# Side work of a two-layer graph-attention kernel issued as 32-column matmuls, four beside each other

## Chip, cores and metric

The kernel runs on one core of a Trainium2 chip. The metric is the device time of one execution in microseconds (us); before the change it is 4478.36 us, the median of 3 runs (4476.70 to 4484.94). All data and all matmuls spoken of here are 32-bit floats unless a line says otherwise.

## What is computed

Input `x` has 8 batches of 2048 rows by 256 features; `adj` is one 2048 x 2048 mask for all batches. Two layers follow each other, each on the normalised and rectified rows of the layer before, each with 4 heads of 64.

```python
# layer 0
h = relu(layernorm(x))
q, k, v = h @ Wq.T + bq, h @ Wk.T + bk, h @ Wv.T + bv        # 4 heads of 64
scores = where(mask == 0, -10, clip(q . k / 8, -10, 10))     # keys in chunks of 256
ctx = sum over chunks of softmax(scores in the chunk) @ v
x = x + (layernorm(ctx @ Wo.T + bo + h) * gamma + beta)
# layer 1
h = relu(layernorm(x));  q = h @ W                            # 4 heads of 64
e = leaky(q . a_src [row] + q . a_dst [column], 0.2)
x = x + elu(softmax(where(mask, e, -9e15)) @ q)
```

## The kernel before

Layer 0 runs over 256 steps (`steps`: 8 batches, 4 blocks of 512 queries, 8 chunks of 256 keys). In each step TensorE makes the scores of a step that lies two ahead (`scores`, L396, contraction over 64 rows, two heads beside each other), VectorE clips and masks them (L404), ScalarE takes the exponential (L410), GpSimd adds two key tiles (L680), and TensorE multiplies the exponentials of the present step with `v` (`weigh`, L416) and sums them with ones (`add_up`, L427). These last two are matmuls with only 32 columns of weights. Four of them are issued in a row, one for each head, and write partitions 0-31, 32-63, 64-95 and 96-127 of the same accumulator. The sums go to ScalarE (L434), through DRAM (`divide`, `spread`) and come back as a factor `r`, with which VectorE scales the contexts (`accumulate`, L452).

Layer 1 runs over 32 passes (8 batches, 2 pairs of heads, 2 halves of the rows) of 16 rounds (`rounds`). A round makes two tiles of weights on VectorE (`clipped`, L761), contexts on TensorE (`weigh_rows`, L772, again four matmuls of 32 columns beside each other), and every second round a sum of them (ScalarE L874, GpSimd L878, TensorE `add_up_rows`, L784).

Everything else is side work, written as generators that wait in a list `aside`. `advance()` lets one or several of them take their next piece, and the main loops call it at fixed places: in layer 0 twice in a step, once after the first half of the contexts (between L416 and the next L396) and once after the second half; in layer 1 once in a round. The order on every engine is the order in which the program issues, so that a piece of side work stands in each engine's queue just where `advance()` was called. The side work on TensorE is:

- `turn` (L171): four 128 x 128 transposes of a normalised row pair into `hT`, 64 times in each layer; ScalarE copies the result (L172).
- `block` (L297): the projections to q and k, two matmuls of 128 columns of weights and 512 moving columns for each half, 128 times in layer 0 (16 of them at the start, before the steps). ScalarE copies the result (L304).
- `sides` (L191): four matmuls with 256 moving columns, 64 times for v in layer 0 (ScalarE copies, L314) and 64 times for q of layer 1 (VectorE multiplies, L629).
- `finish` (L479): four matmuls with 256 moving columns for the output projection of layer 0, 64 times (VectorE adds, L487).
- `preparation` (L599): four transposes, 8 times; `ending` (L805, four transposes of the sums, 32 times; VectorE takes their reciprocal at L807) and (L815, four transposes of the contexts, 64 times; VectorE L818).
- a small matmul in `preparation` (L559), which has 32 columns of weights already and 128 moving columns.

All side work shares one accumulator (`aux`, one buffer after the start), so that a piece waits until the copy of the piece before it is done. At the last pass of each batch of layer 1, `drain` issues what is left of the next batch's preparation, its last L191 pieces among it, in a row.

The lines of the side work before are full matmuls or transposes with all 128 columns of weights, as here in `sides`:

```python
            for ic in range(FC):
                nc.tensor.matmul(
                    ps[:, u, :],
                    hT[:, ic, t * P : (t + 1) * P],
                    rhs[:, ic, :],
```

Of the kernel before, what the change touches and what calls it, by code (L numbers as in the profile page):

```python
# [16 lines left out]
P = 128  # L17
# [34 lines left out]
def layers(  # L52
# [18 lines left out]
    nc = tc.nc  # L71
# [81 lines left out]
    def normal(xb, blk, two, norm):  # L153
# [9 lines left out]
            hs.append(h)  # L163
        return hs

    def turn(hs, two, hT):

        ps = aux().rearrange("p (t c r) -> p c t r", t=2, c=FC)
        for u in range(2):
            for c in range(FC):  # L170
                nc.tensor.transpose(ps[:, c, u, :], hs[u][:, c * P : (c + 1) * P], ident)  # L171
        nc.scalar.copy(  # L172
            hT[:, :, two * 256 : (two + 1) * 256].rearrange("p c (t r) -> p c t r", t=2), ps
        )
# [10 lines left out]
    def sides(rhs, two, hT):  # L185

        ps = aux().rearrange("p (t f) -> p t f", t=2)
        for u in range(2):
            t = 2 * two + u
            for ic in range(FC):  # L190
                nc.tensor.matmul(  # L191
                    ps[:, u, :],
                    hT[:, ic, t * P : (t + 1) * P],
                    rhs[:, ic, :],
                    start=(ic == 0),
                    stop=(ic == FC - 1),
                )
        return ps
# [78 lines left out]
    def block(b, blk, xb, qs, ks, vs):  # L277

        first = b and (b - 1) * NQB * NCH

        while b and here[0] < first + (NCH, 2 * NCH, 3 * NCH, 4 * NCH - 2)[blk]:
            yield False
        while b == 1 and len(made) < NQB:
            yield False
        if b and blk == 0:
            yield True
        hT = big.tile([P, FC, QB], F32, tag="hT", name="hT", bufs=1)
        yield from block_turned(xb, blk, norm_of[b], hT)
        for name, to in (("q", qs), ("k", ks)):
            if name == "q":  # L290
                r = big.tile([P, FC, QB], F32, tag="q", name="qT", bufs=4)
            else:
                r = big.tile([P, FC, QB], F32, tag="kv", name="kT", bufs=12)
            for oc in range(FC):
                ps = aux()
                for ic in range(FC):
                    nc.tensor.matmul(  # L297
                        ps,
                        wT[name][:, ic, oc * P : (oc + 1) * P],
                        hT[:, ic, :],  # L300
                        start=(ic == 0),
                        stop=(ic == FC - 1),
                    )
                nc.scalar.activation(  # L304
                    r[:, oc, :], ps, AF.Identity, bias=bcol[name][:, oc : oc + 1], scale=PART[name]
                )
                if oc == FC - 1:
                    to.append(r)
                yield
        while b and here[0] < first + (0, 0, 3 * NCH + 2, 3 * NCH + 4)[blk]:  # L310
            yield False
        r = big.tile([P, NT, F], F32, tag="kv", name="v", bufs=12)
        for two in range(NT // 2):
            nc.scalar.copy(r[:, 2 * two : 2 * two + 2, :], sides(wT["v"], two, hT))  # L314
            if two == 1:
                vs.append(r)
            yield
# [24 lines left out]
    for name, w in (("q", Wq), ("k", Wk), ("v", Wv), ("o", Wo)):  # L342
# [14 lines left out]
        for ic in range(FC):  # L357
            ps = aux()[:, :F]
# [97 lines left out]
    def finish(b, qb, acc):  # L456
        rstd, off = norm_of[b]
        xb = load(x[b], qb)
        n = here[0]

        while here[0] < n + 1:
            yield False
        o = big.tile([P, NT, F], F32, tag="o", name="o")
        for t in range(NT):
            i = qb * NT + t
            nc.scalar.activation(
                o[:, t, :], xb[:, t, :], AF.Relu, scale=rstd[:, i : i + 1], bias=off[:, i : i + 1]
            )
        nc.gpsimd.tensor_tensor(o, o, bcast(brow["o"], 1, NT), ALU.add)
        yield True  # L470
        while here[0] < n + 2:
            yield False
        mv = small.tile([P, NT, 2], F32, tag="mv2", name="mv2")
        for two in range(NT // 2):
            ps = aux().rearrange("p (t f) -> p t f", t=2)
            for u in range(2):
                t = 2 * two + u
                for part in range(2):
                    nc.tensor.matmul(  # L479
                        ps[:, u, :],  # L480
                        acc[:, part, t * P : (t + 1) * P],
                        wT["o"][:, part, :],
                        start=(part == 0),
                        stop=(part == 1),
                    )
            mine = o[:, 2 * two : 2 * two + 2, :]
            nc.vector.tensor_tensor(mine, mine, ps, ALU.add)  # L487
            yield
            for u in range(2):
                t = 2 * two + u  # L490
                row_stats(nc, small, mv[:, t, :], o[:, t, :])
        rstd2 = small.tile([P, NT], F32, tag="rstd2", name="rstd2")
        off2 = small.tile([P, NT], F32, tag="off2", name="off2")
        roots(mv, rstd2, off2, slice(0, NT))
        yield True
        offsets(rstd2, off2, slice(0, NT))
        n = here[0]
        while here[0] < n + 1:
            yield False
        for t in range(NT):  # L500
            nc.scalar.activation(
                o[:, t, :], o[:, t, :], AF.Identity,
                scale=rstd2[:, t : t + 1], bias=off2[:, t : t + 1],
            )
            if t == 1:
                yield True
        for k, more in enumerate((bcast(brow["gamma"], 1, NT), bcast(brow["beta"], 1, NT), xb)):
            yield True
            n = here[0]
            while here[0] < n + 1:  # L510
                yield False
            nc.gpsimd.tensor_tensor(o, o, more, ALU.add if k else ALU.mult)
        nc.gpsimd.dma_start(
            x1[b][qb * QB : (qb + 1) * QB, :].rearrange("(t p) f -> p t f", p=P), o
        )
        yield True
# [27 lines left out]
    def preparation(b):  # L544
# [4 lines left out]
        er = const.tile([P, NQB, P], F32, tag="wv", name="er")  # L549
# [46 lines left out]
        yield True  # L596
        ps = aux().rearrange("p (b k) -> p b k", k=P)
        for blk in range(NQB):
            nc.tensor.transpose(ps[:, blk, :], er[:, blk, :], ident)  # L599
        ed = ps.rearrange("p b (c k) -> p (b c) k", k=32)[:, :, H : 2 * H]  # L600
        far = small.tile([P, NKT, H], F32, tag="far", name="far")
        nc.vector.scalar_tensor_tensor(far, ed, -0.8, bcast(off_s, 1, NKT), ALU.mult, ALU.add)
# [193 lines left out]
    def ending(k, cT, dT):  # L796

        b, hp, half = passes[k]
        xs = big.tile([P, 2, NT, P], F32, tag="acc", name="xh")
        for blk in range(2):  # L800
            nc.sync.dma_start(xs[:, blk, :, :], mine(x1[b], 2 * half + blk, hp))
        yield True
        ps = aux().rearrange("p (c k) -> p c k", c=NT)
        for c in range(NT):
            nc.tensor.transpose(ps[:, c, :], dT[:, c * P : (c + 1) * P], ident)  # L805
        r = small.tile([P, 2, NT, 2], F32, tag="inverse", name="inverse")
        nc.vector.reciprocal(r, ps.rearrange("p c (h b k) -> p b c h k", h=2, b=2)[:, :, :, :, 0])  # L807
        nc.vector.tensor_reduce(
            inverse_most[:, k : k + 1], r.rearrange("p b c h -> p (b c h)"), mybir.AxisListType.X, ALU.max
        )  # L810
        yield
        for blk in range(2):
            ps = aux().rearrange("p (t f) -> p t f", t=NT)
            for t in range(NT):
                nc.tensor.transpose(ps[:, t, :], cT[:, blk, t * P : (t + 1) * P], ident)  # L815
            both = big.tile([P, 2, NT, P], F32, tag="c", name="z")
            z, low = both[:, 0, :, :], both[:, 1, :, :]
            nc.vector.tensor_tensor(  # L818
                z.rearrange("p t (h d) -> p (t h) d", h=2),
                ps.rearrange("p t (h d) -> p (t h) d", h=2),  # L820
                bcast(r[:, blk, :, :].rearrange("p c h -> p (c h)"), 2, DH),
                ALU.mult,
            )
            yield

            xh = xs[:, blk, :, :]
            nc.scalar.activation(low, z, AF.Relu, scale=-1.0)
            nc.scalar.activation(low, low, AF.Exp, scale=-1.0)
            nc.scalar.activation(z, z, AF.Relu)
            nc.scalar.activation(xh, xh, AF.Copy, bias=-1.0)  # L830
            yield True
            nc.gpsimd.tensor_tensor(z, z, low, ALU.add)
            nc.gpsimd.tensor_tensor(xh, xh, z, ALU.add)
            yield True
            nc.sync.dma_start(mine(out[b], 2 * half + blk, hp), xh)
# [365 lines left out]
```

## Time and profile before

| | us |
|---|---|
| median of 3 runs | 4478.36 (4476.70 to 4484.94) |
| the profiled execution | 4470.84, of which span 4469.0 |
| layer 0 in the trace (starts of the first and last of its sums, L427) | 126 to 2885 |
| layer 1 in the trace (starts of the first and last L761) | 2908.5 to 4444.4 |

The mean granted clock of TensorE is 0.991. In the trace a 32-bit matmul leaves two records for its matmul and two for its weight load; a transpose leaves one of each. The groups of the side work on TensorE, with the columns "busy us, mean ns of one | idle before, and its releaser":

```profile
L479 PE MATMUL aux<-wo,acc 128*128 128x256 f32 x512 | 128.2, 393 | 0.0
L191 PE MATMUL aux<-wv,hT 128*128 128x256 f32 x512 | 126.1, 390 | 0.0
L297 PE MATMUL aux<-hT,wk 128*128 128x512 f32 x256 | 125.5, 615 | 0.0
L171 PE MATMUL aux<-ident,h 128*128 128x128 f32 x512 | 92.3, 297 | 28.4 <-ACT h L160 27.3
L815 PE MATMUL aux<-ident,cT 128*128 128x128 f32 x256 | 42.3, 288 | 1.1 <-DVE z L818 0.8 <-DVE inverse L807 0.4
L805 PE MATMUL aux<-ident,dT 128*128 128x128 f32 x128 | 21.0, 286 | 0.7 <-ACT dT L892 0.7
L559 PE MATMUL aux<-hT,wa 128*32 128x128 f32 x512 | 20.5, 273 | 0.0
```

The form "128*128" is rows times columns of the weights; "128x256" is partitions by moving columns. A duration holds the time that a matmul spends passing through the array, which overlaps the next one, so what a block of them costs is read from start to start, not from these means.

### The profile page before, as it was taken

To read this page: it belongs to the slowest core of one execution; us is meant where nothing else is said; L and a number is where in the kernel's file an instruction comes from. 1 tells how busy PE (TensorE), PEld (TensorE's weight loads), DVE (VectorE), ACT (ScalarE), POOL (GpSimd) and SP (SyncE) were. 2 spreads that over 40 slices of the span, in tenths; PEclk is the share of its full clock that TensorE was granted. 3 is DMA by queue.
4 is the path that set the end of the run, shared out by engine and by line. 5 is a ranking of instruction groups with operands and counts; after the bars stand their busy time and mean duration, and the time that the engine had idled before them with its cause. 6 is when DMAs were issued, how large, how long until landed. Compare 5 with 4: busy or idle time off the path is not lost. (4 is left out here: it accounts for less than half of the span.)

```text
span 4469.0 us, 73769 instructions
## 1 busy us (share of the span) xinstructions
PE 4235.0 (95%) x28598; PEld 1462.8 (33%) x28598; DVE 3157.1 (71%) x3736; ACT 2712.5 (61%) x3454; POOL 3275.9 (73%) x1558
## 2 busy tenths in 40 slices
PE   6799999999999999999999999989999999999998
PEld 3233333323323333333333333323233332323332
DVE  1775566566565565575565566588989889898987
ACT  4766556656655665665656557565647566565755
POOL 0477787787677777777777777777877777787877
PEclk8999999999999999999999999999999999999999
DMA  2421121111121121121111122121221212122111
GB/s 70 140 62 44 43 66 47 43 56 56 35 64 54 37 66 44 46 64 44 47 55 50 40 64 61 44 100 50 72 63 60 78 57 86 52 74 62 59 55 35
DMA packets 295000, 262.03 MB, mean 59 GB/s; under 512 B 96240, under 2 KB 245488, under 8 KB 294640
## 3 DMA queue, kind: packets, MB, share of 16 engines
q1 hardware_dynamic: 290032, 240.45, 18.8%
q0 software_dynamic: 4608, 16.78, 1.0%
q8 instruction: 226, 3.70, 0.3%
q14 instruction: 134, 1.10, 0.1%
HBM read 218.83 MB, written 36.18 MB: 57 GB/s over the span
## 5 line engine op out<-in xcount | busy, mean ns | idle before, releaser
L680 POOL TENSOR_TENSOR add<-E 128x1024 f32<-128x1024 f32 x512 | 1201.3, 2369 | 721.9 <-PE sums L427 532.1
L410 ACT ACTIVATE E<-E 128x1024 f32<-128x1024 f32 x1024 | 1080.5, 1057 | 827.3 <-DVE E L404 809.6
L404 DVE SCALAR_TENSOR_TENSOR E<-big,limit 128x1024 f32<-128x1024 f32 x1024 | 1203.7, 1217 | 521.6 <-PE big L396 515.5
L761 DVE SCALAR_TENSOR_TENSOR e<-near,far,limit 128x1024 f32<-128x1024 f32 x1024 | 1240.0, 1273 | 23.2 <-ACT near L750 9.8
L878 POOL TENSOR_TENSOR t<-t,e 128x1024 f32<-128x1024 f32 x448 | 1054.4, 2387 | 246.0 <-ACT t L874 210.4
L416 PE MATMUL both<-E,v 128*32 128x512 f32 x8192 | 1037.7, 601 | 59.8 <-DVE c L452 42.3
L772 PE MATMUL acc<-e,qn 128*32 128x512 f32 x8192 | 1060.7, 597 | 24.4 <-DVE e L761 13.5
L396 PE MATMUL big<-qT,kT 64*128 64x512 f32 x4096 | 1032.3, 620 | 11.8 <-DVE E L404 11.8
L874 ACT ACTIVATE t<-e,quot 128x1024 f32<-128x1024 f32 x512 | 561.2, 1142 | 313.5 <-PE den L784 173.0
L396 PEld LDWEIGHTS big<-qT,kT 64*128 64x128 f32 x4096 | 351.6, 187 | 572.0 <-issue 348.8
L454 POOL TENSOR_TENSOR acc<-acc,c 128x1024 f32<-128x1024 f32 x224 | 532.9, 2379 | 3.6 <-DVE c L452 3.6
L452 DVE TENSOR_TENSOR c<-both,r 128x1024 f32<-128x1024 f32 x224 | 274.2, 1224 | 345.9 <-PE both L416 157.1
L416 PEld LDWEIGHTS both<-E,v 128*32 128x32 f32 x8192 | 214.7, 109 | 752.3 <-issue 572.8
L772 PEld LDWEIGHTS acc<-e,qn 128*32 128x32 f32 x8192 | 259.2, 109 | 591.5 <-issue 451.1
L784 PE MATMUL den<-t,for_sums 128*32 128x512 f32 x2048 | 347.6, 595 | 30.6 <-POOL t L878 29.8
L427 PE MATMUL sums<-add,ones 128*32 128x512 f32 x2048 | 269.1, 592 | 0.2 <-POOL add L680 0.2
L434 ACT COPY s<-sums 128x512 f32<-128x512 f32 x256 | 148.4, 580 | 75.5 <-PE sums L427 71.3
L784 PEld LDWEIGHTS den<-t,for_sums 128*32 128x32 f32 x2048 | 79.2, 110 | 223.1 <-issue 113.3
L191 PE MATMUL aux<-w,hT 128*128 128x256 f32 x512 | 127.6, 392 | 22.6 <-DVE qn L629 22.6
L160 ACT ACTIVATE h<-x,off,rstd 128x256 f32<-128x256 f32 x256 | 139.2, 593 | 4.3 <-DMA x<-in_x_dram 2.3
L297 PE MATMUL aux<-hT,wq 128*128 128x512 f32 x256 | 135.7, 658 | 2.7 <-ACT hT L172 2.7
L479 PE MATMUL aux<-wo,acc 128*128 128x256 f32 x512 | 128.2, 393 | 0.0
(117 smaller groups left out, 3033.8 us busy)
## 6 DMA issues: line engine op xcount, KB each, us to landing
r<-inv SPq DMA_DIRECT2D x1024, 64.0 KB
x<-in_x_dram SPq DMA_DIRECT2D x92, 512.0 KB
x<-x SPq DMA_DIRECT2D x64, 512.0 KB
es<-er SPq DMA_DIRECT2D x64, 512.0 KB
adj_in<-in_adj_dram SPq DMA_DIRECT2D x32, 512.0 KB
x<-o POOLq DMA_DIRECT2D x32, 512.0 KB, 3.9
xh<-x SPq DMA_DIRECT2D x64, 256.0 KB
out_dram<-xh SPq DMA_DIRECT2D x64, 256.0 KB
```

What stands on the lines that cost most here:

```text
L396: nc.tensor.matmul(ps[:, hh, :], ks[kt // NT][own, hp, (kt % NT) * P : (kt % NT + 1) * P], qs[qb][own, hp, :], start=True, stop=True,)
L404: nc.vector.scalar_tensor_tensor(e, ps, -0.5, bcast(limit[:, qb, kt, :], 1, 2), ALU.max, ALU.min)
L410: nc.scalar.activation(e, e, AF.Exp, scale=0.25 * EDGE)
L416: nc.tensor.matmul(both[32 * h : 32 * h + 32, part, :], vs[kt // NT][:, kt % NT, mine], es[h // 2][:, h % 2, :], start=first, stop=not first,)
L452: nc.vector.tensor_tensor(to, both, bcast(r, 1, 2), ALU.mult)
L454: nc.gpsimd.tensor_tensor(acc, acc, to, ALU.add)
L680: nc.gpsimd.tensor_tensor(both, first[hp], second[hp], ALU.add)
L761: nc.vector.scalar_tensor_tensor(e, near[hh], far[:, jt, h : h + 1], limit[:, 2 * half : 2 * half + 2, jt, :], ALU.max, ALU.min,)
L772: nc.tensor.matmul(acc[32 * q : 32 * q + 32, blk, :], qn[jt // NT][:, jt % NT, hp * P + 32 * q : hp * P + 32 * q + 32], es[q // 2][:, blk, :],
L784: nc.tensor.matmul(den[32 * q : 32 * q + 32, :], for_sums[:, m, 2 * hp + q // 2, :], ts[q // 2][:, q % 2, :], start=(m == 0 and k == 0), s ...
L874: nc.scalar.activation(t, now[hh], AF.Copy, scale=quot[:, jt // 2, h : h + 1])
L878: nc.gpsimd.tensor_tensor(ts[hh], ts[hh], now[hh], ALU.add)
```

## The change

A helper cuts a matmul's weights into four slices of 32 columns, each writing its own 32 partitions of the accumulator. All projections use it. All 32-bit transposes of the side work use it too, as a real matmul with the identity as moving operand in place of the transpose operation. The 16-bit transposes of the mask (L260), the transposes of the weights at the start (L360), and the code of the second path for unusual inputs, which doesn't run here, stay. The other engines' instructions and their order are the same; on TensorE 1952 side matmuls and transposes become 7808.

```diff
+    def narrow(to, lhsT, rhs, start, stop):
+        for j in range(0, P, 32):
+            nc.tensor.matmul(to[j : j + 32], lhsT[:, j : j + 32], rhs, start=start, stop=stop)
+
+    def flip(to, tile):
+        narrow(to, tile, ident, True, True)
+
     def turn(hs, two, hT):
...
-                nc.tensor.transpose(ps[:, c, u, :], hs[u][:, c * P : (c + 1) * P], ident)
+                flip(ps[:, c, u, :], hs[u][:, c * P : (c + 1) * P])
...
@@ sides
-                nc.tensor.matmul(
+                narrow(
                     ps[:, u, :],
                     hT[:, ic, t * P : (t + 1) * P],
...
@@ block
-                    nc.tensor.matmul(
+                    narrow(
                         ps,
                         wT[name][:, ic, oc * P : (oc + 1) * P],
...
@@ finish
-                    nc.tensor.matmul(
+                    narrow(
                         ps[:, u, :],
                         acc[:, part, t * P : (t + 1) * P],
...
@@ preparation
-            nc.tensor.transpose(ps[:, blk, :], er[:, blk, :], ident)
+            flip(ps[:, blk, :], er[:, blk, :])
...
@@ ending
-            nc.tensor.transpose(ps[:, c, :], dT[:, c * P : (c + 1) * P], ident)
+            flip(ps[:, c, :], dT[:, c * P : (c + 1) * P])
...
-                nc.tensor.transpose(ps[:, t, :], cT[:, blk, t * P : (t + 1) * P], ident)
+                flip(ps[:, t, :], cT[:, blk, t * P : (t + 1) * P])
```

## The prediction

> **What bounds the kernel now.** I read the page first: the engines' totals, the slices and the chain.
>
> ```profile
> PE 4235.0 (95%) x28598; PEld 1462.8 (33%) x28598; DVE 3157.1 (71%) x3736; ACT 2712.5 (61%) x3454; POOL 3275.9 (73%) x1558
> ...
> PE   6799999999999999999999999989999999999998
> PEld 3233333323323333333333333323233332323332
> DVE  1775566566565565575565566588989889898987
> ...
> PE 18%; DVE 8%; POOL 3%; issue 3%; ACT 1%; POOLq 0%; ACTq 0%; DVEq 0%
> ```
>
> TensorE (PE) is at nine tenths nearly everywhere, but VectorE (DVE) goes from 5 or 6 tenths in layer 0 to 8 or 9 in layer 1. So the layers need separate sums. The table by stages says the same (columns: us, then busy us and count of PE, weight loads, DVE, ScalarE, GpSimd, then clock, DMA share, GB/s):
>
> ```profile
> 130.00:2860.00 2730.00, 2634.79 (x15986) 907.39 (x15986) 1715.60 (x2148) 1677.98 (x2118) 2002.57 (x917) 1.00 0.19 55
> 2910.00:4400.00 1490.00, 1416.58 (x11608) 475.72 (x11611) 1340.70 (x1449) 917.76 (x1170) 1177.41 (x585) 1.00 0.22 65
> ```
>
> In layer 0 PE is busy 97% and nobody else over 73%. In layer 1 PE shows 95% and DVE 90%, but a PE record includes passage through the array, so PE's real load is less. Next the timeline of PE in layer 0 (start us, length us, line, count of records), read from start to start:
>
> ```profile
> 636.24 1.99 PE L396 MATMUL big<-qT,kT 64*128 64x512 f32 x8
> 638.16 1.06 PE L416 MATMUL both<-E,v 128*32 128x512 f32 x8
> 639.04 1.04 PE L427 MATMUL sums<-add,ones 128*32 128x512 f32 x8
> 639.90 1.04 PE L416 MATMUL both<-E,v 128*32 128x512 f32 x8
> 640.87 1.98 PE L297 MATMUL aux<-hT,wq 128*128 128x512 f32 x4
> 642.78 1.99 PE L396 MATMUL big<-qT,kT 64*128 64x512 f32 x8
> 644.70 1.92 PE L416 MATMUL both<-E,v 128*32 128x512 f32 x16
> 646.56 1.98 PE L297 MATMUL aux<-hT,wk 128*128 128x512 f32 x4
> 648.47 1.99 PE L396 MATMUL big<-qT,kT 64*128 64x512 f32 x8
> ```
>
> Four 32-column matmuls of 512 moving columns (8 records) take 0.86 us (639.04 to 639.90) when more of the kind follow, but 0.97 (639.90 to 640.87) when a 128-column block follows: 0.11 us is lost at the change of form. Two 128-column matmuls of the same size take 1.91 (640.87 to 642.78), where two groups of four would take 1.72. The same place in layer 1, with a 32-column block of 128 moving columns (L559) and transposes (L171):
>
> ```profile
> 3188.54 1.92 PE L772 MATMUL acc<-e,qn 128*32 128x512 f32 x16
> 3190.28 0.62 PE L559 MATMUL aux<-hT,wa 128*32 128x128 f32 x16
> 3190.72 1.90 PE L772 MATMUL acc<-e,qn 128*32 128x512 f32 x16
> ...
> 3195.80 0.66 PE L171 MATMUL aux<-ident,h 128*128 128x128 f32 x4
> 3196.39 1.92 PE L772 MATMUL acc<-e,qn 128*32 128x512 f32 x16
> 3198.13 1.04 PE L784 MATMUL den<-t,for_sums 128*32 128x512 f32 x8
> 3199.10 0.66 PE L171 MATMUL aux<-ident,h 128*128 128x128 f32 x4
> ```
>
> The 16 records of L559 take 0.44 us, 0.11 for each set of four. Four transposes take 0.59 (3195.80 to 3196.39), and the L784 before one pays the 0.11 (0.97 for 0.86). Last, what DVE waits for, since it leads in layer 1 (us in total, times, longest):
>
> ```profile
> DVE qn L629 <- PE aux L191: 79.8, 55, 2.9
> DVE inverse L807 <- PE aux L805: 61.9, 32, 9.0
> ```
>
> Both are waits for side work of PE.
>
> **What the Trainium skill says.** "TensorEngine Tiling (Array Packing)", Tiling Modes, Key Properties: "Changing tiling mode (not just tile) drains the TensorE". The trace agrees: 0.97 for 0.86 above. "TensorE: Matmul & The Clock Gate", Part 3, The mechanism: matmuls on different column tiles run at the same time, starts about 4 ns apart. Here the starts of the four records of a set lie 6 to 7 ns apart, and the sets 429 ns (half of 0.858). "FP8 and Floating Point Precision", TensorE Precision Notes: true 32-bit multiplication takes four passes. The trace shows two records for each matmul and one for each transpose, so a transpose turned into a matmul doubles its streaming: 2 x 0.109 for 0.109 us. The tiling page's Gotcha 2 (Restrictions and Gotchas) excludes transpose mode of 32-bit data under column tiling, which is why that doubling can't be had back; no run here shows it.
>
> **The change, part by part.** The medians below are over all blocks of a kind in the trace with the same neighbours, start to start.
>
> *Projections to q and k (L297).* Before: 1.914 us. After: four sets of 0.429 = 1.716. The loss at the change of form (0.114) is paid by L416 before, and in future by the narrow block, whose next is L396: once in either case. Gain 0.198. In the steps of layer 0 there are 112 such blocks: 22.2 us. (The other 16 are at the start.)
>
> *L191 and L479 (256 moving columns).* Before: 1.924. After: eight sets. The trace has no 32-column set of 256; half of the one of 512 is 0.215 and twice that of 128 is 0.218; below neither can it stream, and above it could expose its weight loads, which take 0.13 us for four (L427's loads). I take 0.215, 1.72 in all, gain 0.20. In the steps there are 62 of L479 and 61 of L191: 24.6 us.
>
> *Transposes in layer 0 (L171, 64 in the steps).* Before 0.585, after eight sets of 0.109 = 0.872: loss 0.287, in all 18.4 us. The upper end is a set that exposes its loads, 0.24; no lower end under 0.109.
>
> Is that on the path? From sum to sum (L427) a step with two L297 blocks takes 12.23 us in all 41 cases, without any idle time on PE, and one with one L479 10.33 (median of 17); the bare step of 8.40 is seen too, but its median is 8.81, because contexts there wait for the factor `r` (PE waits 42.3 us for DVE c and 17.3 for acc in all). The gain falls in the full steps, so it is real time. The cover of `r` is gone only in bare steps, where nothing is gained; full steps have 1.5 us or more over 8.81. The loss of L171 falls partly into lighter steps: those with two L171 have 0.32 us of idle time on the mean, and half of the pieces stand between the sums and the next contexts, in the shadow of `r`. I take a fifth of the loss off: 15. Layer 0: -22.2 - 24.6 + 15 = -32 us; without that cover -28.
>
> *Start.* 8 L171, 16 L297 and 8 L191, next to 16-bit transposes of 128 columns. PE waits for ScalarE and DMA there; the longer transposes lie on a chain (ACT h, PE, ACT hT), about 8 x 0.3 = +2, the projections give back 1 to 2. Taken as +1.
>
> *Layer 1.* Next to 32-column work both changes of form go away: one block of transposes costs 0.872 for 0.585 + 0.114, so +0.173; a block of L191 1.72 for 1.924 + 0.114, so -0.32. But DVE sets the pace: two L761 take 2.39 us a round (1.19 each, start to start), PE's contexts and sums 2.15. So I count only where DVE stands for PE. In the batch from 3099 to 3293 these places are:
> - at each of four L807, DVE waits 1.1 to 2.7 us for L805. From the start of the transposes to the last result is 0.655 before; after it is 7 x 0.109 + 0.02 + 0.27 = 1.055; with the 0.114 ahead saved, +0.29. Four: +1.15.
> - from 3184 to 3214 PE never rests (before the wait of 2.7); five L171 lie there: 5 x 0.173 = +0.87. One L599 before the last L807: +0.17. The other L171 and L815 end in slack (DVE waits for L815 1.6 us in the whole run; PE waits 0.8 for GpSimd at 3238).
> - from 3258 to 3293 L191 is on the chain: four blocks amid contexts, 4 x -0.32 = -1.28, and two L815, +0.35; then four in the drain, each waiting for DVE's multiply of the last. There only the way to the result counts: 1.99 before, 7 x 0.215 + 0.40 = 1.91 after, -0.09; and the last saves its change back, -0.2. Together -0.55.
>
> Sum +0.7 a batch. Seven batches have a preparation within: +5. The last has four L807 alone, +1; the first preparation's L191 at the end of layer 0 -2. Layer 1: +4, from -6 (its L191 count fully) to +13 (all of PE's: (56 + 32 + 64 + 7) x 0.173 - 28 x 0.32 - 28 x 0.2 = +13).
>
> *More instructions.* PE's records grow from 57,196 to about 82,500 (5,952 of side work become 31,232), and each has to be fetched. The page shows 3.70 MB in 226 packets on the queue for instructions; that would grow by 25,280/57,196, 44%. PE shows no wait for it now, and sets of four at this density run in L559 without a gap; I cost it at nothing. What would show is idle PE before narrow blocks put down to "issue".
>
> Sum: -32 + 1 + 4 = -27 on the profiled execution's 4470.8, that is 4444 there; it stands 7.5 below the median of the runs, so 4451 for the median.
>
> **Rivals.**
>
> *The gain is hidden.* If steps of layer 0 fall back on the wait for `r`, or layer 1 pays the full +13 and the start more, what is left is about -10: 4468. For it: 557 ns of idle in the mean bare step; GpSimd 73%. Against: no idle PE time at all in steps with two projections.
>
> *Slower: the sets of 128 expose their weight loads.* L559 has four sets in a row; a transpose block has eight, with 64 instructions in 0.87 us and 32 loads of 110 ns each. If half of the sets wait for their loads (0.13), a block costs 0.52 more. On the path are 64 blocks of layer 0 and some 12 in each of 7 batches, 148: +77, so 4528. The gain is gone at 27/(148 x 8) = 0.023 us for each set, 0.132 for 0.109. Against: L559 at 0.109 flows on into L772 without loss, its next loads issued ahead.
>
> *More is gained.* If the transposes hide (layer 0 has shadow under `r`, layer 1 slack in its stretches) it is -47 in layer 0 and -6 in layer 1: 4425. Against: L171 in full steps has no shadow, and L807 waits for PE every time.
>
> **How the numbers follow.** Forecast (4440 to 4463) 0.67; hidden 0.14; slower 0.09; more gained 0.10. The predicted time is that of the first, 4451. The range 4432 to 4472 leaves out half of the larger gain, the slower case and a little of the hidden one. A change of under 0.2% (9 us) can't be told from none: the hidden case lies about this bound, and gives half of its share to each side. Faster 0.84, same 0.07, slower 0.09.
>
> **What would show it.** In the profile after: a step with two L297 at 11.83 us instead of 12.23; L297's block (16 narrow records) 1.72 and L416 before it 0.86; a block of L171 (32 narrow records) 0.87 before other 32-column work; L172's wait for it longer by 0.3; the wait of DVE at L807 up from 61.9 to about 90, and at L629 down from 79.8 to about 65. It would be wrong if sets of 128 or 256 columns lie further apart than 0.11 and 0.215, if PE shows idle time within narrow blocks, or if layer 1's span (L761, 2908.5 to 4444.4) moves by more than 13.

## The result

The changed kernel takes 4456.24 us (median of 6 runs, 4452.34 to 4459.91), the kernel before 4478.15 (6 runs, 4474.90 to 4484.94): ratio 0.9948, 95% interval 0.9935 to 0.9961, or 21.9 us less. The forecast was 4451. The profiled execution has a span of 4452.5 us, 16.5 less than the one before. The profiles show less gain than the medians because the profiled execution of before (4470.84) is 7.3 us under the median of its kernel, that of the changed kernel (4454.33) only 1.9.

First the page of the changed kernel: totals, and the queue for instructions (packets, MB, share of 16 engines).

```profile
PE 4213.6 (95%) x41238; PEld 1554.1 (35%) x41238; DVE 3155.0 (71%) x3736; ACT 2713.1 (61%) x3454; POOL 3282.6 (74%) x1558
...
q8 instruction: 325, 5.32, 0.5%
```

The other engines have the same instructions in nearly the same time. TensorE has 12,640 more pairs of records. The instructions fetched grew from 3.70 to 5.32 MB, by 44% as worked out.

The timeline of TensorE in layer 0, at the same place of the program as the one shown of before (lines moved: scores L404, contexts L424, sums L435, narrow side work L169):

```profile
628.19 1.06 PE L169 MATMUL aux<-ident,h 128*32 128x128 f32 x32
629.18 1.99 PE L404 MATMUL big<-qT,kT 64*128 64x512 f32 x8
...
636.58 1.07 PE L424 MATMUL both<-E,v 128*32 128x512 f32 x8
637.47 1.04 PE L435 MATMUL sums<-add,ones 128*32 128x512 f32 x8
638.33 1.04 PE L424 MATMUL both<-E,v 128*32 128x512 f32 x8
639.18 1.90 PE L169 MATMUL aux<-hT,wq 128*32 128x512 f32 x16
641.01 1.99 PE L404 MATMUL big<-qT,kT 64*128 64x512 f32 x8
642.93 1.92 PE L424 MATMUL both<-E,v 128*32 128x512 f32 x16
644.67 1.90 PE L169 MATMUL aux<-hT,wk 128*32 128x512 f32 x16
646.50 1.99 PE L404 MATMUL big<-qT,kT 64*128 64x512 f32 x8
648.42 1.06 PE L424 MATMUL both<-E,v 128*32 128x512 f32 x8
649.30 1.04 PE L435 MATMUL sums<-add,ones 128*32 128x512 f32 x8
```

The contexts before a projection now take 0.86 us (638.33 to 639.18; 0.97 before), the projection 1.83 (639.18 to 641.01; 1.91 before), of which 0.11 is the change of form towards the scores. From sum to sum the step is 637.47 to 649.30, 11.83 us, where it was 12.23. A block of L171 takes 0.99 (628.19 to 629.18), 0.11 of it the change.

By stage, in us (starts of the first and last sums bound layer 0; starts of the first and last clip, L761 before and L769 after, bound layer 1; the last record of the sums of before starts at 2893.8, not at 2885, as the table of the times before has it):

| | before | changed |
|---|---|---|
| up to the first sums | 125.8 | 125.6 |
| layer 0 | 2768.0 | 2747.2 |
| last sums to first clip | 14.6 | 18.3 |
| layer 1 | 1535.9 | 1535.4 |
| after the last clip | 24.6 | 26.1 |

All of the gain is in layer 0; layer 1 as a whole takes as long as it did.

### The profile page after: what moved, and what is told of

Read it like the earlier page. It is cut to its first block, busy times and chain, and to the rows that moved or that the text cites. A ratio compares the mean times of both kernels' runs of the same rounds, so it can differ in the third digit from the quotient of the medians.

```text
span 4452.5 us, 99059 instructions
## 1 busy us (share of the span) xinstructions
PE 4213.6 (95%) x41238; PEld 1554.1 (35%) x41238; DVE 3155.0 (71%) x3736; ACT 2713.1 (61%) x3454; POOL 3282.6 (74%) x1558
## 3 DMA queue, kind: packets, MB, share of 16 engines
q8 instruction: 325, 5.32, 0.5%
## 5 line engine op out<-in xcount | busy, mean ns | idle before, releaser
L769 DVE SCALAR_TENSOR_TENSOR e<-near,far,limit 128x1024 f32<-128x1024 f32 x1024 | 1240.2, 1273 | 23.8 <-ACT near L758 9.5
L780 PE MATMUL acc<-e,qn 128*32 128x512 f32 x8192 | 1116.1, 594 | 30.5 <-DVE e L769 19.6
L424 PE MATMUL both<-E,v 128*32 128x512 f32 x8192 | 1036.6, 600 | 67.2 <-DVE c L460 46.2
L404 PE MATMUL big<-qT,kT 64*128 64x512 f32 x4096 | 1034.0, 621 | 12.8 <-DVE E L412 12.8
L404 PEld LDWEIGHTS big<-qT,kT 64*128 64x128 f32 x4096 | 351.7, 187 | 594.2 <-issue 344.6
L780 PEld LDWEIGHTS acc<-e,qn 128*32 128x32 f32 x8192 | 319.9, 110 | 544.9 <-issue 400.2
L424 PEld LDWEIGHTS both<-E,v 128*32 128x32 f32 x8192 | 215.2, 109 | 758.5 <-issue 572.7
L792 PE MATMUL den<-t,for_sums 128*32 128x512 f32 x2048 | 373.3, 596 | 24.7 <-POOL t L886 24.6
L435 PE MATMUL sums<-add,ones 128*32 128x512 f32 x2048 | 268.8, 592 | 0.2 <-POOL add L688 0.2
L169 PE MATMUL aux<-ident,h 128*32 128x128 f32 x4096 | 158.5, 281 | 25.5 <-ACT h L160 25.4
L169 PEld LDWEIGHTS aux<-ident,h 128*32 128x32 f32 x4096 | 130.8, 112 | 95.2 <-ACT h L160 54.4
L792 PEld LDWEIGHTS den<-t,for_sums 128*32 128x32 f32 x2048 | 90.6, 110 | 206.3 <-issue 107.7
L169 PE MATMUL aux<-w,hT 128*32 128x256 f32 x2048 | 134.1, 380 | 23.4 <-DVE qn L637 23.4
```

The lines of the kernel that those rows point to most:

```text
L169: nc.tensor.matmul(to[j : j + 32], lhsT[:, j : j + 32], rhs, start=start, stop=stop)
L404: nc.tensor.matmul(ps[:, hh, :], ks[kt // NT][own, hp, (kt % NT) * P : (kt % NT + 1) * P], qs[qb][own, hp, :], start=True, stop=True,)
L424: nc.tensor.matmul(both[32 * h : 32 * h + 32, part, :], vs[kt // NT][:, kt % NT, mine], es[h // 2][:, h % 2, :], start=first, stop=not first,)
L769: nc.vector.scalar_tensor_tensor(e, near[hh], far[:, jt, h : h + 1], limit[:, 2 * half : 2 * half + 2, jt, :], ALU.max, ALU.min,)
L780: nc.tensor.matmul(acc[32 * q : 32 * q + 32, blk, :], qn[jt // NT][:, jt % NT, hp * P + 32 * q : hp * P + 32 * q + 32], es[q // 2][:, blk, :],
L792: nc.tensor.matmul(den[32 * q : 32 * q + 32, :], for_sums[:, m, 2 * hp + q // 2, :], ts[q // 2][:, q % 2, :], start=(m == 0 and k == 0), s ...
```

## Experiments

Each ratio is to runs of the kernel before on the same chip; stages are compared between single profiles. In layer 0 one profile is good to some us only: projections alone and the kernel of experiment 2 have all but the same instructions there, and took 2715.8 and 2719.4 us. Layer 0 waits there for the factor `r`, which comes through DRAM; the fifth experiment takes this wait out.

### 1. Projections alone, transposes alone

```diff
@@ projections alone
     def flip(to, tile):
-        narrow(to, tile, ident, True, True)
+        nc.tensor.transpose(to, tile, ident)
@@ transposes alone: sides, block, finish
-                narrow(
+                nc.tensor.matmul(
```

> Only the projections (q, k, v, layer 1's q, output) in 32 columns; all transposes as before. Theory (the sums of the prediction: same form saves 0.2 us a projection block, a real matmul costs 0.29 us a transpose block in layer 0 and 0.17 in layer 1): steps with two projections keep 11.83 us, steps with L171 lose nothing; layer 0 shorter by 38 us (46.8 less some 8 to 9 that bare steps give to the wait for r), layer 1 by 5: about 4436, ratio 0.990. Rival (the change of form is what counts, and side work of mixed forms gives it back): no better than the changed kernel, 4456 or more.

> Only the transposes in 32 columns as real matmuls; projections full. Theory: layer 0 longer by 15 to 18 us, layer 1 by 15 to 20 (0.29 at each of 32 L807, 0.17 at each L171 of the stretch in which PE never rests): about 4510, ratio 1.007. Rival (the transposes hide in the shadow of r and in VectorE's lead): within 5 us of before, 4483 or less.

Measured: projections alone 4412.93 us against 4471.05, ratio 0.9872 (0.9857 to 0.9888); transposes alone 4499.42, ratio 1.0057 (1.0044 to 1.0071). So the change has two halves of opposite sign, as the sums had it, and the rivals of both runs fall. Together the halves make -0.71% of the time, against -0.52% for the whole change; with intervals of 0.13 to 0.16% either way on each of the three ratios, that they simply add up is not excluded, nor shown. Stages against those of before: projections alone layer 0 -52.2, layer 1 -11.5; transposes alone layer 0 +17.9, layer 1 +10.1. The first came out better than the ratio of 0.990 expected of it: I had taken off 8 to 9 us for gain given back in bare steps, and it wasn't given back; and I had put layer 1 at 5, less than half of what the prediction's own terms for its projections give (12.8). The second cost a little less than its 1.007, since layer 1 lost 10.1 us and not 15 to 20.

In the timeline of projections alone, transposes keep their old form between 32-column groups and pay both changes (622.28 to 623.26 is 0.97 for the contexts, 623.26 to 623.84 is 0.59 for four transposes):

```profile
622.28 1.04 PE L424 MATMUL both<-E,v 128*32 128x512 f32 x8
623.26 0.66 PE L172 MATMUL aux<-ident,h 128*128 128x128 f32 x4
623.84 1.99 PE L404 MATMUL big<-qT,kT 64*128 64x512 f32 x8
...
632.13 1.04 PE L435 MATMUL sums<-add,ones 128*32 128x512 f32 x8
632.99 1.04 PE L424 MATMUL both<-E,v 128*32 128x512 f32 x8
633.85 1.90 PE L169 MATMUL aux<-hT,wq 128*32 128x512 f32 x16
635.68 1.99 PE L404 MATMUL big<-qT,kT 64*128 64x512 f32 x8
```

Together 0.97 + 0.59 = 1.56, against 0.86 + 0.99 = 1.84 with narrow transposes: the 0.29 of the prediction. Of the kernels that do the whole computation this is the fastest, 1.3% under the one before.

### 2. Where the transposes cost: layer 1 alone

```diff
-                flip(ps[:, c, u, :], hs[u][:, c * P : (c + 1) * P])
+                if in_layer_1[0]:
+                    flip(ps[:, c, u, :], hs[u][:, c * P : (c + 1) * P])
+                else:
+                    nc.tensor.transpose(ps[:, c, u, :], hs[u][:, c * P : (c + 1) * P], ident)
```

> Projections in 32 columns, transposes in 32 columns in layer 1 alone (turn of layer 0 and of its last part as before; er, sums and contexts narrow). Theory: layer 0 as in projections only, -38, layer 1 as in the changed kernel, about 0 to +1: 4440. Rival (layer 1's transposes cost nothing there, VectorE sets the pace): equal to projections only, within 2 us.

Measured: 4423.40 us, ratio 0.9896 (0.9881 to 0.9912), on the same chip as projections alone. Layer 0 is 2719.4 (projections alone 2715.8), layer 1 1535.0 (1524.4). So narrow transposes in layer 1 cost 10.5 us there, and as much in the medians of the two kernels; the rival, that VectorE hides them, falls. The run is better than the 4440 expected of it because layer 0 gained 48.6 us, not 38.

### 3. Slices of 64 columns

```diff
-        for j in range(0, P, 32):
-            nc.tensor.matmul(to[j : j + 32], lhsT[:, j : j + 32], rhs, start=start, stop=stop)
+        for j in range(0, P, 64):
+            nc.tensor.matmul(to[j : j + 64], lhsT[:, j : j + 64], rhs, start=start, stop=stop)
```

> All side work in slices of 64 columns, two beside each other, in place of 32 and four. Theory (the gain of a projection is the change of form that goes away): contexts have 32 columns, so both changes of form are back; a step with two L297 near 12.2 us, projections gain about nothing and transposes lose 0.3 to 0.4 a block: slower than before, 4500 to 4520. Rival (the gain comes from smaller weight loads that are issued ahead, whatever the form): L297 steps at 11.83, about 4456.

Measured: 4516.30 us, ratio 1.0105 (1.0089 to 1.0120). Timeline of this kernel:

```profile
640.63 1.04 PE L435 MATMUL sums<-add,ones 128*32 128x512 f32 x8
641.49 1.04 PE L424 MATMUL both<-E,v 128*32 128x512 f32 x8
642.46 1.94 PE L169 MATMUL aux<-hT,wq 128*64 128x512 f32 x8
644.33 1.99 PE L404 MATMUL big<-qT,kT 64*128 64x512 f32 x8
```

The contexts pay the change again (641.49 to 642.46, 0.97), and the projection takes 1.87 (642.46 to 644.33). Of the 1.91 for full width only 0.05 is gained. A step with two L297 takes 12.14 us. So of the 0.20 that 32 columns gain for a block, 0.15 comes with the neighbour's form, and only 0.05 with smaller weights as such.

The weight loads (PEld) of the projections shown above tell where the rest is, first before, then in the changed kernel:

```profile
640.87 0.30 PEld L297 LDWEIGHTS aux<-hT,wq 128*128 128x128 f32 x2 [0.84 <-ACT s L434]
```

```profile
638.76 0.13 PEld L169 LDWEIGHTS aux<-hT,wq 128*32 128x32 f32 x4 [0.30 <-issue]
```

Before, the first load starts together with its block (640.87), and from the block's first record to its second 0.534 us pass in place of 0.429. In the changed kernel the first loads start 0.43 ahead of the block (639.18), and its sets follow each other at 0.429. With 64 columns the loads start with the block again (642.46), but they are shorter (0.133 for 0.186), and the first set takes 0.480. So the 0.20 is made up of the change ahead of the block (0.114) and of a first load that isn't hidden (0.105), less 0.02, by which the four slices of a set start one after another.

A block of L171 in 64 columns takes 1.02 (median over the 64 of layer 0) in place of 0.585, with the change ahead of it besides. Layer 0 is 8.9 us longer than before, layer 1 29.4.

### 4. The second record of a transpose, without the narrow form

```diff
     def flip(to, tile):
-        narrow(to, tile, ident, True, True)
+        nc.tensor.matmul(to, tile, ident, start=True, stop=True)
```

> Projections in 32 columns; the transposes are real matmuls with the identity, but with all 128 columns. It parts the two costs of a narrow transpose: the second record, and the form. Theory (a real full matmul has weight loads of 190 ns, longer than its stream of 109): a block of L171 takes 8 x 0.19 and the changes of form, some 1.7 us, against 0.87 for narrow and 0.585 for the transpose operation; time 4500 to 4530. Rival (only the second record costs; loads stay hidden): a block takes 8 x 0.11 + 0.15 = 1.03, time about 4470.

Measured: 4490.59 us, ratio 1.0032 (1.0020 to 1.0045). Timeline:

```profile
628.45 1.04 PE L424 MATMUL both<-E,v 128*32 128x512 f32 x8
629.43 1.16 PE L172 MATMUL aux<-ident,h 128*128 128x128 f32 x8
630.51 1.99 PE L404 MATMUL big<-qT,kT 64*128 64x512 f32 x8
```

The block takes 1.09 us (629.43 to 630.51), not 1.7: the theory of this run falls. Its rival (1.03) is nearly right about the block, though its time of 4470 is 20 us too low. Within the block, weight loads with a duration of 192 ns start 0.11 us apart, at the pace of the streams, without holding them up. Of the 0.50 by which the block is longer than four transposes (0.585), four more streams of 0.109 are 0.44. The common form takes 0.10 of it back where scores follow (0.99) and 0.22 where 32-column work follows (0.87), and in both cases the 0.11 ahead of the block. So what a narrow transpose costs is its second record. Layer 1 takes 1568.8 us here, 32.9 over before and 44.4 over projections alone. Layer 0 is 18.4 shorter than before, near the -14.7 that its blocks make in sum (-46.8 for projections, 64 times 0.50 for transposes).

### 5. Layer 0 without the way of r through DRAM

The factor `r`, for which bare steps of layer 0 wait, is replaced by a constant in three kernels: before, changed, and projections alone. The division by the sums of exponentials is left out, with its reciprocals on VectorE and its transfers.

```diff
-        got = small.tile([P, 16], F32, tag="sum", name="sum")
-        nc.sync.dma_start(got, s[0:P:32, :].rearrange("h (j i) -> h j i", i=16))
-        return got
+        return s
...
     def spread(got):
-        nc.vector.reciprocal(got, got)
...
-        return r
+        return fixed
```

> The kernel before without the way of the factor r through DRAM: contexts are scaled by a constant 0.1 (the division by the sums of exponentials is left out; the sums are still made on TensorE and copied by ScalarE). It is the base for the next two. Both theories: bare steps of layer 0 fall from a median of 8.8 us to about 8.4, layer 0 shorter by 20 to 45 us than 2768.

> The changed kernel, in the same way without r (the division is left out). Theory A (the saved time of layer 0 is real, and some of it, and of the 18 us of the transposes' extra, only shifts into waits for r): with no such waits layer 0 is shorter than that of e5_no_r_before by 28 us, within 3. Theory B (something else in the changed kernel costs 8 us, say fetching instructions or slower scores): the difference stays at 21 us or less.

> The kernel with narrow projections alone, without r (the division is left out). Theory A: layer 0 shorter than that of e5_no_r_before by 47 us, within 3. Theory B (projections alone gain 52 because of something the sums don't hold): 52 or more here too.

Measured (median of 2 runs each): 4391.89, 4362.03 and 4331.86 us. Layer 0 in their profiles: 2692.9, 2666.5 (-26.5) and 2646.2 (-46.7). The base fell by 75, more than the 20 to 45 expected: the 76 bare steps came to a median of 8.40 as expected and give 47 of it (697.9 us to 650.5 in sum), but the steps with one L479 alone had waited too (194.7 us to 180.1 for 17), and a few others. The two differences are those of theory A (-28 and -47, each within 3). They leave some 2 us at most for anything else in the changed kernel's layer 0, the fetching of instructions included. Projections alone had -52 with `r`, so I put the 5 over the sum down to the waits for `r`. Layer 1, in which `r` plays no part, repeats the earlier runs: 1533.4, 1533.6 and 1523.1 us.

## Why the prediction was right

**The blocks came out as worked out.** A step with two L297: 11.83 forecast, 11.835 measured in all 41. A 32-column set of 256 columns, for which the trace of before had no row: 0.215 taken, and the block of L191 and L479 takes 1.840 with the change of form (median of 62 and 56), so (1.840 - 0.114) / 8 = 0.216. A transpose block: 0.872 forecast; 0.873 where the next work has 32 columns, 0.987 before scores. The slower rival, sets that expose their loads, has nothing for it; where transposes stand among 32-column work in layer 1, the eight sets run without a gap. ScalarE's wait for L171 grew from 34.4 us in 29 waits to 45.6 in 43, so that most of the 128 pieces still find slack there and don't show the 0.3 named.

**Layer 0: -32 forecast, -20.8 in the one profile, -26.5 with the wait for r taken out.** The step that was off is "I take a fifth of the loss off: 15". There was no cover for L171. Without `r` the transposes cost 2666.5 - 2646.2 = 20.2 us, the full 18.4 and two more; in the profile of transposes alone 17.9, and 31.4 between projections alone and the changed kernel, both with `r`. Leaving the sum uncovered, -28, would have been closer. With `r` in play the rest looks like wait: the steps that hold one L479 and no other side work gained nothing in the profile (194.7 us in all before, 194.7 after, 17 of each), though their projection is 0.2 shorter, and the 76 bare steps took 6.9 more in sum (704.8 for 697.9). Projections alone shows no such loss in bare steps (698.3), so it isn't a fixed share of the gain; what makes it differ from profile to profile was not settled.

**Layer 1: +4 forecast, -0.6 measured.** One term was right and the other nearly twice what it measured. Projections: seven times 1.83, -12.8, and -11.5 measured with projections alone. Transposes: 2.54 a batch and 1 in the last, +19, and +10.1 measured with transposes alone. That the two measured terms come to nothing together was not foreseen. The waits of VectorE within layer 1 (us in total, times, longest), first before, then transposes alone:

```profile
DVE qn L629 <- PE aux L191: 70.2, 49, 2.1
DVE inverse L807 <- PE aux L805: 52.9, 31, 2.7
```

```profile
DVE qn L637 <- PE aux L199: 71.3, 49, 2.1
DVE inverse L815 <- PE aux L169: 59.3, 31, 3.0
```

The wait for the transposed sums grew by 6.4 us in 31 times, 0.21 each in place of 0.29, and that includes the places in which I had added 0.87 for L171. Counted by the starts of the first exponential of each pass (L750), the four passes of a batch change by +0.3, +0.5, +1.0 and -0.2 us in the transposes alone (49.9, 42.2, 44.6, 57.5 before; 50.2, 42.7, 45.5, 57.3 with narrow transposes; medians of the six middle batches). The first three together grow by 1.8, as the prediction's steps have it: three times 0.29 for L807, and 0.87 for the L171 of the stretch where TensorE never rests, 1.74. The step that failed is the fourth pass, with the drain. It gives a little back, where I had counted +0.81 (0.29 for its L807, 0.17 for L599 and 0.35 for two L815): about 1 us in each of seven batches, and so most of the 9 us between +19 and +10.1. Why TensorE's lateness doesn't add up there was not traced; part of what it lost earlier it may have waited for anyway.

The same waits in the changed kernel:

```profile
DVE qn L637 <- PE aux L169: 62.0, 49, 2.1
DVE inverse L815 <- PE aux L169: 55.4, 31, 3.0
```

The wait for L191 falls by 8.2 us in 49 times, 0.17 each. The forecast for the whole run was 79.8 to about 65 for this wait and 61.9 to about 90 for the other; it became 71.5 and 64.5. The second was plainly wrong, and not only by the size above: 32 times 0.29 and, in seven batches, 0.87 + 0.17 are 16.6, so that about 78 would have followed from the prediction's own steps.

**Start: +1 forecast, -0.3 measured.** Between the layers the change measured +3.6 in one profile, where -2 had been counted for L191; without `r` it is -0.8 (11.6 to 10.7). So it seems to belong to the same waits.

**More instructions at no cost:** right within the 2 us of the fifth experiment.

The forecast, 5 us from the measured median, holds because its large terms, 47 for projections and 18 for transposes in layer 0, were read from start to start in the trace. Some of its closeness is luck: in layer 0 it promised too much, in layer 1 too little. And on the profiled execution the miss is 10 us (4454.3 for 4444); the 7.5 us then added for the median were 1.9 for the changed kernel. The prediction didn't draw the conclusion that its own sum held: the transposes' part of the change was a loss in every term, and leaving them as they were brings 0.76% of the time more (ratio 0.9872 for 0.9948), some 34 us.

## What to carry to other kernels

When a matmul stands between others that use a part of the array's columns, give it their form: here the change of form took 0.11 us, and with a first weight load that wasn't hidden a block of full matmuls cost 0.2 us more than the same block in slices of the neighbours' form. Don't do the same to a 32-bit transpose, which left a single record in its own operation and two as a matmul (0.585 us for four, against 0.87 to 0.99); count the records first. And price a change that has two kinds of edits kind by kind, since half of it may pay for the other half.

## What the hardware showed that I had not expected

Weight loads of 192 ns don't hold up streams of 109 ns of the full form; they follow at the stream's pace (experiment 4: 1.09 us for eight). Only the first load of a block of another form shows, 0.105 us of it (experiment 3). And groups of columns can run apart: after a block of narrow transposes in layer 1 of the changed kernel, the records of the next group stand out of step.

```profile
3175.82 1.11 PE L169 MATMUL aux<-ident,h 128*32 128x128 f32 x26
3176.69 0.60 PE L780 MATMUL acc<-e,qn 128*32 128x512 f32 x2
3176.76 0.50 PE L169 MATMUL aux<-ident,h 128*32 128x128 f32 x6
3177.09 1.89 PE L780 MATMUL acc<-e,qn 128*32 128x512 f32 x14
3178.41 1.42 PE L792 MATMUL den<-t,for_sums 128*32 128x512 f32 x8
```

26 of the 32 records of the transposes have started when the first two of the contexts begin, 70 ns ahead of the last six; so two of the four slices have gone on to the contexts while the other two still transpose. That these are groups of columns is read from the count and the order of issue, since a record doesn't name its columns. Nothing is gained or lost by it in total (from 3175.82 to 3179.26, the next such block, 3.44 us for 0.87 + 1.72 + 0.86).
